# SyncE loads 32 table rows a quad instead of 20 in a graph attention kernel

## The chip, the cores and the metric

The kernel runs on one core of a Trainium2 chip. A core has a matrix engine (PE; its weight loads are listed apart as PEld), a vector engine (DVE), a scalar engine (ACT), a general engine (POOL) and a sequencer that only issues transfers and waits (SP). All of them run their own instruction streams in order and meet through semaphores. The metric is the device time of one execution in microseconds (us), as the median of several timed executions.

## The reference

The program is one graph attention layer with a residual. N = 12500 nodes have 128 features, E = 200000 edges come sorted by target node, and there are four heads of 32 channels:

```python
h   = relu(layernorm(x)) @ W_node.T            # a row per node, (H, HD)
e   = edge_features @ W_edge.T
att = sum(concat([h[src], h[dst], e]) * a)     # per edge and head
att = where(att > 0, att, 0.2 * att)
m   = max(segment_max(att, dst), 0)
ex  = exp(att - m[dst])
den = segment_sum(ex, dst) + (E - deg) * exp(-m)
out = x + segment_sum(ex / den[dst] * h[src], dst)
```

What matters here is `h[src]`: for every edge one row of the node table has to come to the edge's place. The sources are random, so each row is 548 scattered bytes (137 numbers of 4 bytes).

## The kernel before, in words

**Tiling.** The edges are cut into 392 groups of 511 (512 places with one carried in front), and four groups make a quad: 98 quads. A group has four chunks of 128 edges, one edge per partition, so a quad has 16 chunks. A first stage normalises the nodes and writes the node table to DRAM; then the quads are worked through.

**Three steps of a quad.** `logits(q, i)` makes the logits of group i of quad q: DVE compares targets (L612), PE multiplies (L618, L621). After some quads (a "super" of mostly four) `softmax` runs over them. `sums(q)` weighs the gathered rows (DVE, L925), marks the targets (DVE, L899) and lets PE add up rows by target (L964, and L841 for the carried row); ACT prepares columns for it (L893, L947), carries a row (L851) and takes the exponent for the division (L871), whose result DVE finishes (L1136). The functions are generators that are interleaved by hand: `together` takes one step of each in turn, so one step of logits of quad q + 5 stands beside one step of sums of quad q. In the late quads the same order holds, with windows of two groups (quads 36 to 74) and then of one (from 75), where earlier quads have one window for all four groups.

**How rows get to the edges.** The usual way is a gather: POOL issues one indirect transfer per chunk (L183). A ring of eight quads holds the rows (`ga`), and the gathers of quad q + 2 are issued when the logits of quad q begin. Some chunks go without a gather. `rows_for` picks them: one chunk of the last group of a quad, every 128 / a_quad quads, where a_quad is the number of rows that an engine is to load per quad. For these chunks `loaded_by_row` issues 128 transfers of one row each (L796), on ACT for one set of chunks and on SP for another. The addresses come from a list of sources (`of`, L782, loaded by SP), which DVE multiplies by the row's size (`at_row`, L789) and from which the engine loads a_quad registers at a time (L538). The rows land in one of three buffers of 128 rows; `take_rows` lets ACT wait for a chunk's count and copy it into the ring (L815) at the beginning of that quad's logits.

**When rows are issued.** `load_rows(by_sync, q, n)` advances SP's generator by n rows. It is called at the end of each of the four steps of logits with `BEHIND_LOGITS`, and at the end of each of the four steps of sums with `BEHIND_HOT`, both from quad 2 on. SP's chunks are set by

```python
sync_rows = rows_for((BEHIND_LOGITS + BEHIND_HOT) * QG, J - 2, SYNC_FROM + 6)
```

so the same two constants give the number of chunks.

**What else is in SP's queue.** SP issues, in the order of the program, the edge features of quad q + 2 (`ea`, L345), its targets (`db`, L351, after the last step of logits of quad q), its target rows (`pw`, L552), the inputs of the next quad (`inputs`, L552), the results (`out_dram`, L552, each waiting for DVE at L1136), rows for the softmax (`dr`, L592), and register loads (L538) for those whose place is computed. All of it, and the rows, run in one line.

Of the kernel before, what the change touches and what calls it, by code (L numbers as in the profile page):

```python
# [38 lines left out]
QUADS = 8  # L39
ROWS_FROM, ROWS_AHEAD, ROW_BUFS = 6, 7, 3  # L40
BEHIND_COUNT, BEHIND_SUMS, BEHIND_QUAD = 5, 1, 4
SYNC_FROM, BEHIND_LOGITS, BEHIND_HOT = 2, 3, 2
CLASSES = (22, 4, NARROW), (36, 4, WIDE), (75, 2, WIDE), (None, 1, NARROW)
FOLDS, PARTS = 1, 3
SETS = max(NODE_T, QG * J)
# [1500 lines left out]
```

## Time and profile before

| | |
|---|---|
| timed executions | 2762.9 us median of 3 (2750.94 to 2772.4) |
| the profiled execution | 2792.17 us, its span 2790.3 us |
| granted PE clock, mean | 0.531 of full speed |
| PE, PEld, DVE, ACT, POOL busy | 49%, 45%, 45%, 12%, 52% |
| rows loaded by ACT, by SP | 2304, 1664 |
| gathers from the table, from x | 1463, 72 |

The profile is of one execution. Its busy shares count work of the engines themselves; what a sequencer does (register loads, waiting, issuing transfers) is not busy time, so SP has no share at all and is read from the order of its issues and from its waits. PE's durations are modelled at full clock, while the clock granted to it is listed beside them. The waits put each idle stretch down to what ended it last; "remote" and "issue" are those where the profile names no engine. 1664 rows are 13 chunks of 128.

### The profile page before, as it was taken

The numbers are of one execution on the slowest core, as the hardware profiler recorded it, in microseconds if no ns is written. First come the engines' busy times: TensorE is split into PE (matmuls) and PEld (weight loads), VectorE is DVE, ScalarE is ACT, GpSimd is POOL, SyncE is SP. The second block draws the span as 40 slices with busy tenths as digits, with TensorE's granted clock in tenths as the row PEclk, the third lists the DMA queues.
The fourth block names the chain that finished last, engine by engine and source line by source line (L and its number), as shares of the span: only waits on it lengthen the run. The fifth ranks groups of instructions, "written<-read, shape, count | busy, mean of one in ns | idle before, by whom it ended". The sixth has DMA issues, their size and how long they took to land. (4 is left out here: it accounts for less than half of the span.)

```text
span 2790.3 us, 33673 instructions
## 1 busy us (share of the span) xinstructions
PE 1375.5 (49%) x7375; PEld 1256.4 (45%) x7375; DVE 1259.5 (45%) x3401; ACT 335.6 (12%) x1114; POOL 1458.8 (52%) x1550
## 2 busy tenths in 40 slices
PE   3655345344335334434555455555555545554565
PEld 3545344334334334434455454445444544443455
DVE  4543344234233334324445445545453553453476
ACT  3533000000000000000000000000000011111112
POOL 6455444544545444454556565565565556556611
PEclk8656555555555555555555555555555555555556
DMA  5533333333323333333444444444443443444430
GB/s 171 158 94 79 83 87 93 92 80 73 107 85 104 95 92 95 92 107 86 112 119 126 115 120 115 124 126 124 118 127 99 108 106 93 109 103 108 111 75 24
DMA packets 158894, 288.27 MB, mean 103 GB/s; under 512 B 62393, under 2 KB 106040, under 8 KB 148305
## 3 DMA queue, kind: packets, MB, share of 16 engines
q1 hardware_dynamic: 103262, 174.80, 20.8%
q0 software_dynamic: 49120, 107.44, 16.6%
q10 hardware_dynamic: 6306, 3.85, 0.6%
q8 instruction: 61, 1.00, 0.2%
q14 instruction: 145, 1.18, 0.2%
HBM read 268.72 MB, written 17.20 MB: 102 GB/s over the span
## 5 line engine op out<-in xcount | busy, mean ns | idle before, releaser
L183 POOL DMA_INDIRECT ga<-table,srci x1463 | 1381.1, 944 | 1177.3 <-PE acc L841 553.7
L964 PE MATMUL acc<-ga,hot 128*113 128x137 f32 (+1 forms) x2702 | 721.3, 442 | 693.3 <-issue 310.0
L964 PEld LDWEIGHTS acc<-ga,hot 128*113 128x113 f32 (+1 forms) x2702 | 595.4, 281 | 719.4 <-issue 323.9
L621 PE MATMUL lg<-wblk,ea 128*128 128x8 f32 x1568 | 406.7, 357 | 0.0
L621 PEld LDWEIGHTS lg<-wblk,ea 128*128 128x128 f32 x1568 | 379.1, 307 | 0.0
L618 PEld LDWEIGHTS <-at 112*128 112x128 bf16 (+1 forms) x1568 | 222.8, 167 | 249.8 <-DVE at L612 152.2
L925 DVE TENSOR_TENSOR ga<-ga,ex_ps 128x528 f32<-128x528 f32 x385 | 265.4, 690 | 20.3 <-PE ex_ps L753 12.7
L618 PE MATMUL lg<-pw,at 112*128 112x12 bf16 (+1 forms) x1568 | 171.0, 182 | 197.4 <-DVE at L612 134.6
L612 DVE TENSOR_TENSOR at<-const_ps,db 112x512 bf16<-112x512 f32 (+1 forms) x392 | 264.5, 675 | 6.9 <-DMA db<-in_dst_dram 5.6
L1124 DVE SCALAR_TENSOR_TENSOR den_of<-acc,den_of 113x4 f32<-113x4 f32 (+1 forms) x114 | 17.9, 157 | 521.9 <-ACT den_of L871 375.8
L899 DVE TENSOR_TENSOR hot<-const_ps,slot 128x448 f32<-128x448 f32 (+1 forms) x392 | 215.2, 550 | 0.0
L841 PE MATMUL acc<-ga,hot 128*81 128x137 f32 (+1 forms) x402 | 134.5, 437 | 106.3 <-ACT ga L851 85.4
L630 DVE TENSOR_REDUCE const_ps<-lg 128x64 f32<-128x192 f32 x98 | 35.2, 360 | 291.8 <-remote 255.3
L841 PEld LDWEIGHTS acc<-ga,hot 128*81 128x81 f32 (+1 forms) x402 | 95.0, 271 | 122.1 <-ACT ga L851 95.1
L871 ACT ACTIVATE den_of<-acc 113x4 f32<-113x4 f32 (+1 forms) x114 | 19.7, 173 | 994.0 <-remote 811.0
L753 PE MATMUL ex_ps<-ident,ex 64*128 64x64 f32 (+3 forms) x112 | 18.8, 317 | 184.7 <-ACT ex L747 146.8
L753 PEld LDWEIGHTS ex_ps<-ident,ex 64*128 64x128 f32 (+3 forms) x112 | 13.9, 210 | 187.6 <-ACT ex L747 148.6
L183 POOL DMA_INDIRECT ga<-in_x_dram,srci x72 | 68.7, 955 | 41.7 <-issue 21.1
L716 DVE TENSOR_TENSOR_SCAN ends<-thru,tops,ex_ps 1x16 f32<-1x16 f32 (+3 forms) x112 | 24.1, 216 | 118.9 <-remote 93.3
L441 PE MATMUL row_ps<-wcat,hT 128*128 128x137 f32 x198 | 45.5, 388 | 51.5 <-DVE hT L433 14.8
L687 DVE TENSOR_TENSOR t_ps<-t_ps,low 64x511 f32<-64x511 f32 (+3 forms) x28 | 19.3, 689 | 113.1 <-ACT low L684 113.1
L851 ACT COPY ga<-acc 1x133 f32<-1x133 f32 x175 | 44.8, 256 | 205.6 <-issue 116.8
(179 smaller groups left out, 1200.2 us busy)
## 6 DMA issues: line engine op xcount, KB each, us to landing
db<-in_dst_dram SPq DMA_DIRECT2D x53, 1024.0 KB
ea<-in_edge_t_dram SPq DMA_DIRECT2D x98, 512.0 KB
by_row<-table ACTq DMA_DIRECT2D x2304, 0.5 KB
db<-in_dst_dram SPq DMA_DIRECT2D x45, 640.0 KB
by_row<-table SPq DMA_DIRECT2D x1664, 0.5 KB
ga<-table,srci POOLq DMA_INDIRECT x1463
table<-row SPq DMA_DIRECT2D x9, 616.5 KB
xt<-in_x_dram SPq DMA_DIRECT2D x9, 576.0 KB
```

The costliest lines, as they stand in the source:

```text
L183: nc.gpsimd.indirect_dma_start(out=ga[:, i, j, 0:width], out_offset=None, in_=rows, in_offset=bass.IndirectOffsetOnAxis(ap=srci[:, g0 + i, ...
L441: nc.tensor.matmul(row_ps[:, t, :ROW], hT[:, t, :], wcat, start=True, stop=True)
L612: nc.vector.tensor_tensor(at[:span, i, :], node_ps[:span, w0 + i // k:w0 + i // k + 1].to_broadcast([span, GE]), db[:span, i, :], op=OP.is ...
L618: nc.tensor.matmul(lg[:, i, j].rearrange("p k h -> p (k h)"), at[:span, i, j * P:(j + 1) * P], sw, start=i + j == 0, stop=False, skip_grou ...
L621: nc.tensor.matmul(lg[:, i, 2 * w:2 * w + 2, 0, :], ea[:, i, w, :], wblk, start=False, stop=True, skip_group_check=True)
L630: nc.vector.tensor_reduce(st[:, :m], LG[q][:, :m].rearrange("p g j k h -> p g j h k"), AX.X, OP.add)
L753: nc.tensor.transpose(ex_ps[:, j * SBG * H:j * SBG * H + R], ex[:R, j * P:(j + 1) * P], ident[:R, :R])
L841: nc.tensor.matmul(acc, hot[:, i, 0, 0:acc.shape[0]], ga[:, i, 0, :], start=False, stop=stop)
L851: nc.scalar.copy(into, before[0:1, 0:R_CNT + 1])
L899: nc.vector.tensor_tensor(hot[:, i, :, 1:1 + span], lane_ps[:, 0:span].unsqueeze(1).to_broadcast([P, J, span]), slot[:, quads[q][0] + i, : ...
L925: engine.tensor_tensor(val, val, weight.unsqueeze(3).to_broadcast([P, J, H, HW]), op=OP.mult)
L964: nc.tensor.matmul(acc, hot[:, i, j, 0:1 + span], ga[:, i, j, :], start=new and j == (1 if carried else 0), stop=i % k > 1 and i % k == k ...
```

## The change

Two constants: SP issues four rows, and not three, at each step of logits, and four, and not two, at each step of sums. That is 4 x 4 + 4 x 4 = 32 rows a quad in place of 4 x 3 + 4 x 2 = 20.

```diff
-SYNC_FROM, BEHIND_LOGITS, BEHIND_HOT = 2, 3, 2
+SYNC_FROM, BEHIND_LOGITS, BEHIND_HOT = 2, 4, 4
```

`rows_for` now picks a chunk every 4 quads and not every 6.4, from quad 12 and not from quad 15: 22 chunks and not 13. Each of the nine chunks that are added loses its gather on POOL, and gets 128 row transfers and one list of sources on SP, one DVE instruction, and one ACT wait and copy. SP loads 32 registers at a time and not 20. Which chunks ACT loads does not change.

## The prediction

> **What bounds the kernel now.** First the page: how long, which engines, and what clock PE was given. Second the same by stretch.
>
> ```profile
> span 2790.3 us, 33673 instructions
> ...
> PE 1375.5 (49%) x7375; PEld 1256.4 (45%) x7375; DVE 1259.5 (45%) x3401; ACT 335.6 (12%) x1114; POOL 1458.8 (52%) x1550
> ...
> PEclk8656555555555555555555555555555555555556
> ```
>
> ```profile
> 300.00:1200.00 900.00, 382.88 (x2093) 355.27 (x2092) 333.02 (x842) 52.08 (x179) 440.02 (x467) 0.50 0.34 92
> 1300.00:2500.00 1200.00, 629.96 (x3301) 575.44 (x3300) 575.47 (x1484) 110.62 (x416) 706.02 (x748) 0.51 0.42 114
> ```
>
> No engine is busy for more than 52%, but PE's durations are modelled at full clock and the granted clock is 0.50 to 0.51. From 1300 to 2500 us the 629.96 us of PE become 629.96 / 0.51 = 1235 us in a stretch of 1200: PE has no time left there (a little is counted twice where matmuls overlap). From 300 to 1200 us it is 382.88 / 0.50 = 766 of 900. So I take PE as the bound of the second half and as nearly that in the first. Third the groups, for who waits for whom.
>
> ```profile
> L183 POOL DMA_INDIRECT ga<-table,srci x1463 | 1381.1, 944 | 1177.3 <-PE acc L841 553.7 <-issue 387.6 <-remote 159.0
> ...
> L612 DVE TENSOR_TENSOR at<-const_ps,db 112x512 bf16<-112x512 f32 (+1 forms) x392 | 264.5, 675 | 6.9 <-DMA db<-in_dst_dram 5.6 <-issue 1.2
> ...
> L947 ACT COPY ga<-xs 128x80 f32<-128x80 f32 x97 | 31.5, 325 | 39.4 <-DMA ga<-table,srci 20.0 <-issue 12.8 <-DMA rows<-in_dst_rows_dram 2.4
> ...
> L642 DVE TENSOR_TENSOR U<-const_ps,ga 128x64 f32<-128x64 f32 x98 | 26.1, 266 | 16.9 <-ACT ga L324 13.0 <-DVE const_ps L630 0.4
> ...
> L815 ACT COPY ga<-by_row 128x137 f32<-128x137 f32 x31 | 9.4, 303 | 103.7 <-issue 103.7
> ...
> L789 DVE TENSOR_SCALAR at_row<-of 1x128 int32<-1x128 int32 x31 | 6.8, 219 | 0.0
> ```
>
> POOL's gathers are not late. POOL itself waits 553.7 us for PE to be done with a ring buffer (L183, behind L841); the first reader of gathered rows, L642, has no gather among what its 16.9 us of waiting are put down to; L947 waits for gathers for 20.0 us in the whole span. Fourth, SP, which has no busy time: its waits from 1300 to 2500 us (the first answer), and from 300 to 1200 (the second), as total, number, longest.
>
> ```profile
> SPq L552 <- DMA pw<-side: 7.9, 10, 1.4
> SPq L552 <- DVE res L1136: 5.8, 3, 2.1
> SPq L552 <- DVE const_ps L630: 4.2, 2, 3.6
> ```
>
> ```profile
> SPq L552 <- DVE const_ps L630: 88.7, 6, 21.2
> SPq L345 <- remote: 80.3, 13, 16.3
> SPq L552 <- DVE res L1136: 52.4, 9, 12.1
> SPq L552 <- DVE at_row L789: 45.5, 3, 21.9
> ```
>
> The second list holds over 260 us of waiting in 900. The first has 33 rows, these three the longest, and adds to some 38 us in 1200: **in the second half SP runs without a pause**, though nobody waits for it but L612, once, for 5.6 us. Whether that is SP's real load decides this case. One quad of its queue, from one load of targets to the next (columns: start, time until the last issue's end, line, transfer, number):
>
> ```profile
> 1912.74 0.36 SPq L351 DMA_DIRECT2D db<-in_dst_dram  x1
> 1913.20 0.87 SPq L796 DMA_DIRECT2D by_row<-table  x3
> 1914.95 0.32 SPq L552 DMA_DIRECT2D inputs<-in_x_dram  x1
> 1915.45 0.34 SPq L552 DMA_DIRECT2D out_dram<-res  x1
> 1915.90 1.20 SPq L796 DMA_DIRECT2D by_row<-table  x2
> 1917.82 0.70 SPq L345 DMA_DIRECT2D ea<-in_edge_t_dram  x1
> 1919.97 0.00 SPq L552 DMA_DIRECT2D pw<-side  x1
> 1921.38 2.84 SPq L796 DMA_DIRECT2D by_row<-table  x3
> 1924.24 0.00 SPq L552 DMA_DIRECT2D inputs<-in_x_dram  x1
> 1924.32 0.55 SPq L796 DMA_DIRECT2D by_row<-table  x2
> 1925.23 0.06 SPq L552 DMA_DIRECT2D pw<-side  x1
> 1925.38 1.40 SPq L796 DMA_DIRECT2D by_row<-table  x3
> 1927.57 0.71 SPq L552 DMA_DIRECT2D out_dram<-res  x1
> 1929.02 7.42 SPq L796 DMA_DIRECT2D by_row<-table  x7
> 1936.54 0.36 SPq L351 DMA_DIRECT2D db<-in_dst_dram  x1
> ```
>
> A quad takes 1936.54 - 1912.74 = 23.8 us. The same kind of row costs 0.87 us for three at one place and 7.42 for seven at another; the same kind of load of inputs is issued in 0.32 us once and in 0.00 once. An issue of 56 KB that takes nothing is not an issue timed at its own moment. The same line, by kind (ns, least, median, most):
>
> ```profile
> L796 SPq MOVE by_row<-table x1664: 2/29/1407, 197.6 to 2496.9; - x185
> L796 SPq DMA_DIRECT2D by_row<-table x1664: 2/228/1394, 197.7 to 2497.0; - x185
> ```
>
> A register move, which touches no queue of transfers, takes 29 ns or up to 1407, and an issue 228 or 2. I read the dear stretches as records that come late and in bunches, so as a matter of the recording and not of SP's work. That is a reading, not a measurement.
>
> **The change, part by part.**
>
> *Removed: nine gathers* (22 chunks for 1664 / 128 = 13). 9 x 0.944 = 8.5 us of POOL go, and their pauses. POOL was waiting for buffers, so this is worth 0; after it POOL waits that much longer for PE. Bound on the other side: the 20.0 us that L947 waited for gathers, with 8.5 us, 28.5 us, if they all stood on the path and went.
>
> *Added: 9 x 128 = 1152 rows on SP, 12 a quad.* Clean price: 0.87 us for three, the last issue 0.23, so (0.87 - 0.23) / 2 = 0.32 a row, 3.8 us a quad. Registers: 32 at a time, not 20; twelve rows with one such load took
>
> ```profile
> 746.18 5.12 SPq L796 DMA_DIRECT2D by_row<-table  x12
> ```
>
> so (5.12 - 0.23) - 11 x 0.32 = 1.4 us a load, 0.07 a register, and 12 more are 0.8. Together 4.6 us a quad. Dear price: the 20 rows of the quad above took 0.87 + 1.20 + 2.84 + 0.55 + 1.40 + 7.42 = 14.3 us, 0.71 each, so 8.6 + 0.8 = 9.4 us. At the clean price SP's whole quad is 20 x 0.32 + 1.4 for rows, about 8 x 0.45 for the other transfers and 1 for their registers (an estimate from 0.32 to 0.36 an issue in the rows above, and the gaps), 12.4 us, and 17 us after the change, of 23.8: hidden behind PE. I take this, 0 us on the path. At the recorded price it is 23.8 + 9.4, and nothing hides it (first rival).
>
> *Queues passed.* The rows stand ahead of SP's loads of targets, features, inputs and results, which are for the next quad or the one after, so each may come 5 us later within a lead of a quad or more. Behind a wait of SP for `at_row` stand these same loads.
>
> *Added on DVE:* nine L789, 9 x 0.219 = 2.0 us; DVE is busy 575.47 us of 1200, so PE hides them (2.0 if not). Nine lists of sources more are nine issues on SP, like those above under 0.4 us each, in its slack.
>
> *Added on ACT:* nine waits and copies L815, 9 x 0.303 = 2.7 us. They stand in the path, as here before the carried row for which PE waits:
>
> ```profile
> 718.75 0.31 ACT L815 COPY ga<-by_row 128x137 f32<-128x137 f32 x1 [3.84 <-issue]
> 718.90 0.23 ACTq L796 DMA_DIRECT2D by_row<-table  x1
> 718.96 0.26 ACT L851 COPY ga<-acc 1x133 f32<-1x133 f32 x1
> ```
>
> The wait itself should be over: counting the calls in the program's order, a chunk's last row is issued 33 calls, of eight a quad, before it is taken, so four quads. The idle 103.7 / 31 = 3.3 us before each L815 is ACT's own issuing; were it new each time, 9 x 3.6 = 33 us.
>
> **Sum**, against the profiled execution: 0 for the gathers, 0 for SP, 0 for DVE, 2.7 for ACT: 2792.2 + 3 = 2795. That execution lies 29 us above the median of the timed ones, so for the median I add the same to it: 2762.9 + 3 = **2766 us**. About 1% is what a measurement of this kernel can tell from no change (2750.94 to 2772.4).
>
> **Rivals.**
>
> 1. *SP becomes the bound* (slower): its recorded pace is its real one. For: 38 us of waits in 1200, 0.8 a quad; L612's 5.6 us. Against: the moves of 1407 ns and issues of 2. It decides once SP's quad is longer than PE's 23.8 us, and it bites when DVE has to wait for targets (L612), after the lead of a quad is used up. Price: 1200 / 23.8 = 50 quads, from (4.6 - 0.8) x 50 - 24 = +166 to (9.4 - 0.8) x 50 - 24 = +406. I take +260, nearer to the low end, as a longer quad lengthens the clean stretches first: 3023 us.
> The Trainium skill, page "Perfetto Trace Analysis", section "What 'DMA-bound' means", calls a program bound by a DMA sequencer where the issuing engine's track is solid with issues; by that rule this rival would be the forecast. The waits of SP agree with it, the lack of waits for SP does not.
> Its page "NOTIFIC — the notification-queue block", section "10. Constraints, capacities, measured rates", says that writing such records costs an engine no cycles. By it the dear stretches would be SP's own and the sum would be 3023 too; no row here can show which.
>
> 2. *SP is late only in part*: half of the dearness is real. SP's quad is then (12.4 + 23.8) / 2 = 18.1 before, and with (4.6 + 9.4) / 2 = 7 more 25.1: over by 1.3, x 50 - 24 = +41, and up to +100 where the late quads, with more transfers each, are over by more. Taken: +70, 2833 us.
>
> 3. *Faster*: gathers are on the path after all, and all 28.5 us go: 2734 us. For: L947's 20.0 us. Against: 553.7 us of POOL waiting for buffers.
>
> 4. *It does not do what it says.* The counts follow from the same constants, so this is no more than a chunk.
>
> **Chances.** Hidden, 2766 (own range 2750 to 2785): 0.55. SP the bound, 3023: 0.25. In part, 2833: 0.14. Faster, 2734: 0.06. So faster by over 1% 0.06, within 1% 0.55, slower by over 1% 0.39. The range takes the first case, the third, and the lower half of the second: 2742 to 3030, which leaves out about 0.16.
>
> **What would show it.** L183 x1454, SP's rows x2816, L815 and L789 x40. If I am right, the median stays within 1%, L612's wait for targets stays small in the timed pace, and PE's busy time over clock still fills the second half. SP's waits from 300 to 1200 us should shrink. If the first rival is right, L612 waits for `db` by tens or hundreds of us between 1300 and 2500, the clock being the same, and quads there last 27 us or more. What would make me wrong beside these: a wait of ACT at L815 that is new, with PE behind it at L841.

## The result and the profile after

The changed kernel takes 2977.57 us (median, 2961.45 to 2984.73) where the kernel before takes 2767.65 us (2750.94 to 2779.68): a ratio of 1.074, 95% interval 1.0667 to 1.0814. It is slower by 210 us. The profiled execution took 2961.45 us, 169 us more than the profiled one of before. In the experiments further below, the same kernel before took 1981 to 1984 us and not 2767, so their times are compared only with each other; what differs there is part of the finding.

First the page of the changed kernel, for the same lines as before.

```profile
span 2959.7 us, 36007 instructions
...
PE 1370.6 (46%) x7375; PEld 1251.7 (42%) x7375; DVE 1264.6 (43%) x3410; ACT 337.3 (11%) x1123; POOL 1449.7 (49%) x1541
...
PEclk8656555555555555555555555555555555555556
```

Every engine does nearly the same work as before (nine gathers fewer, nine copies more) at the same clock, and the span is longer: the time went into waiting. The table of two stretches says which half it went to.

```profile
300.00:1200.00 900.00, 375.76 (x2085) 350.85 (x2085) 332.36 (x843) 52.05 (x179) 434.25 (x461) 0.51 0.33 92
1300.00:2500.00 1200.00, 562.12 (x2940) 512.70 (x2939) 517.27 (x1336) 95.56 (x356) 627.77 (x667) 0.50 0.36 102
```

From 300 to 1200 us PE gets nearly as much done as before (375.76 us of work against 382.88). From 1300 to 2500 it gets 562.12 done, not 629.96. The groups of the changed kernel, with their idle time and what ended it, name the wait:

```profile
L183 POOL DMA_INDIRECT ga<-table,srci x1454 | 1372.1, 944 | 1356.1 <-PE acc L841 742.3 <-issue 374.7 <-remote 153.4
...
L612 DVE TENSOR_TENSOR at<-const_ps,db 112x512 bf16<-112x512 f32 (+1 forms) x392 | 265.1, 677 | 367.8 <-DMA db<-in_dst_dram 359.4 <-issue 8.2
...
L947 ACT COPY ga<-xs 128x80 f32<-128x80 f32 x97 | 31.4, 324 | 24.2 <-DMA ga<-table,srci 12.9 <-issue 6.8 <-DVE kp L665 0.4
...
L815 ACT COPY ga<-by_row 128x137 f32<-128x137 f32 x40 | 11.7, 302 | 85.8 <-issue 72.1 <-DVE hot L899 6.0 <-DVE at_row L789 5.4
```

L612, which compares targets, waits 359.4 us for the load of `db`; before it was 5.6. POOL waits more for PE, not less, so the gathers aren't late. ACT idles less before L815 than before (85.8 us and not 103.7, with nine copies more), so no new wait for rows shows. How L612's wait reaches PE stands at L618, which multiplies what L612 made; first the kernel before, then the changed one.

```profile
L618 PE MATMUL lg<-pw,at 112*128 112x12 bf16 (+1 forms) x1568 | 171.0, 182 | 197.4 <-DVE at L612 134.6
L618 PE MATMUL lg<-pw,at 112*128 112x12 bf16 (+1 forms) x1568 | 170.3, 181 | 445.7 <-DVE at L612 362.4
```

`db` is issued by SP. SP's waits from 1300 to 2500 us, the three longest of the list:

```profile
SPq L552 <- DMA pw<-side: 4.3, 6, 0.7
SPq L538 <- DVE U L642: 1.8, 1, 1.8
SPq L552 <- DMA inputs<-in_x_dram: 1.4, 2, 0.7
```

The list names next to nothing that SP waits for (17 us in all), and now others wait for SP. How complete such a list is in these two traces is taken up further below. How long its round is follows from the loads of `db` in the same stretch (one line of the source; least, median and longest duration in ns, first and last start); first the kernel before, then the changed one.

```profile
L351 SPq DMA_DIRECT2D db<-in_dst_dram x47: 2/347/712, 1310.3 to 2489.2; - x47
```

```profile
L351 SPq DMA_DIRECT2D db<-in_dst_dram x42: 2/362/785, 1316.3 to 2489.0; - x42
```

Before, (2489.2 - 1310.3) / 46 = 25.6 us a quad; after, (2489.0 - 1316.3) / 41 = 28.6. One quad of SP's queue in the changed kernel, the middle left out:

```profile
1909.38 0.01 SPq L351 DMA_DIRECT2D db<-in_dst_dram  x1
1910.11 3.57 SPq L796 DMA_DIRECT2D by_row<-table  x4
...
1916.98 1.25 SPq L796 DMA_DIRECT2D by_row<-table  x4
...
1924.26 4.96 SPq L796 DMA_DIRECT2D by_row<-table  x4
...
1934.33 8.03 SPq L796 DMA_DIRECT2D by_row<-table  x12
1942.46 0.36 SPq L351 DMA_DIRECT2D db<-in_dst_dram  x1
```

Dear and cheap stretches stand side by side as before: four rows take 1.25 us here and 4.96 there.

### The profile page after: what moved, and what is told of

Same layout as the page of the kernel before. It is cut to its first block, busy times and chain, and to the rows that moved or that the text cites. A ratio compares the mean times of both kernels' runs of the same rounds, so it can differ in the third digit from the quotient of the medians.

```text
span 2959.7 us, 36007 instructions
## 1 busy us (share of the span) xinstructions
PE 1370.6 (46%) x7375; PEld 1251.7 (42%) x7375; DVE 1264.6 (43%) x3410; ACT 337.3 (11%) x1123; POOL 1449.7 (49%) x1541
## 5 line engine op out<-in xcount | busy, mean ns | idle before, releaser
L183 POOL DMA_INDIRECT ga<-table,srci x1454 | 1372.1, 944 | 1356.1 <-PE acc L841 742.3
L964 PE MATMUL acc<-ga,hot 128*113 128x137 f32 (+1 forms) x2702 | 719.5, 442 | 691.4 <-issue 278.1
L964 PEld LDWEIGHTS acc<-ga,hot 128*113 128x113 f32 (+1 forms) x2702 | 594.3, 280 | 716.9 <-issue 292.6
L618 PEld LDWEIGHTS <-at 112*128 112x128 bf16 (+1 forms) x1568 | 217.8, 165 | 503.9 <-DVE at L612 389.5
L612 DVE TENSOR_TENSOR at<-const_ps,db 112x512 bf16<-112x512 f32 (+1 forms) x392 | 265.1, 677 | 367.8 <-DMA db<-in_dst_dram 359.4
L618 PE MATMUL lg<-pw,at 112*128 112x12 bf16 (+1 forms) x1568 | 170.3, 181 | 445.7 <-DVE at L612 362.4
L183 POOL DMA_INDIRECT ga<-in_x_dram,srci x72 | 68.6, 953 | 41.2 <-issue 21.1
L874 ACT COPY pt<-acc 81x137 f32<-81x137 f32 x88 | 23.7, 269 | 344.4 <-PE acc L841 151.9
```

The source lines that it names most:

```text
L183: nc.gpsimd.indirect_dma_start(out=ga[:, i, j, 0:width], out_offset=None, in_=rows, in_offset=bass.IndirectOffsetOnAxis(ap=srci[:, g0 + i, ...
L612: nc.vector.tensor_tensor(at[:span, i, :], node_ps[:span, w0 + i // k:w0 + i // k + 1].to_broadcast([span, GE]), db[:span, i, :], op=OP.is ...
L618: nc.tensor.matmul(lg[:, i, j].rearrange("p k h -> p (k h)"), at[:span, i, j * P:(j + 1) * P], sw, start=i + j == 0, stop=False, skip_grou ...
L964: nc.tensor.matmul(acc, hot[:, i, j, 0:1 + span], ga[:, i, j, :], start=new and j == (1 if carried else 0), stop=i % k > 1 and i % k == k ...
```

## The experiments

**More rows, fewer rows.** The first two change only the constants, to 24 and to 28 rows a quad:

```diff
-SYNC_FROM, BEHIND_LOGITS, BEHIND_HOT = 2, 4, 4
+SYNC_FROM, BEHIND_LOGITS, BEHIND_HOT = 2, 3, 3     # 24 rows
+SYNC_FROM, BEHIND_LOGITS, BEHIND_HOT = 2, 3, 4     # 28 rows
```

> 24 rows a quad on SP, three at each step of logits and of sums: 16 chunks by rows. The changed kernel pays 4.9 us in each quad from about quad 48 to quad 88, for 12 rows more than before. Theory A (SP's issuing is the bound, at its recorded pace of about 0.7 to 0.8 us a row, and SP had some spare time before): there is a threshold. Twelve rows at 0.78 us are 9.4 us, of which 4.9 came through, so 4.5 us a quad were spare; four rows at 0.78 are 3.1 us, less than that, so no loss: 2740 to 2790 us. Theory B (the copies on ACT, the waits for a chunk, or the register loads cost it, so the price goes by the chunk): three of nine chunks, a third of +210: about 2835 us. Theory C (SP had only the 0.8 us a quad of waits that the profile of before shows, and a row costs 5.7 / 12 = 0.47 us): +1.1 us in 40 quads, about 2810 us.

> 28 rows a quad on SP, three at each step of logits and four at each of sums: 19 chunks by rows. Theory A (threshold at 4.5 us a quad, 0.78 us a row): eight rows are 6.2 us, 1.7 over, in some 40 quads +70: about 2835 us. Theory B (by the chunk): six of nine, two thirds of +210: about 2905 us. Theory C (0.8 us spare, 0.47 us a row): +3.0 us in 40 quads, about 2885 us.

Measured: the kernel before 1981.66 us; 24 rows 1979.23 (ratio 0.9984, 0.9972 to 0.9995), 28 rows 1982.75 (1.0007, 0.9993 to 1.002). No loss shows at all, where 32 rows cost 1.0% at this pace (next run), so at this pace nothing goes by the chunk (B, a third and two thirds of it) or by a flat price of every row (C). The 0.2% that 24 rows gain is less than executions of one kernel differ by (1976.45 to 1986.23 us for the kernel before). The 70 us that A gave 28 rows don't show either: its spare time was reckoned from another pace, since the kernel before takes 786 us less here. So the first reading is of the pace itself: the rows on SP in the kernel with 24.

```profile
L796 SPq MOVE by_row<-table x2048: 29/29/38, 136.5 to 1767.1; - x187
L796 SPq DMA_DIRECT2D by_row<-table x2048: 227/228/581, 136.5 to 1767.2; - x187
```

A register move takes 29 to 38 ns and never 1407, an issue 227 to 581 and never 2. The dear stretches and the issues of nothing are gone together, and with them 28% of the time.

**The changed kernel at this pace.** It was run again as it is.

> The changed kernel again, unchanged. In the runs of 24 and 28 rows the kernel before took 1981 us, where it had taken 2767 us in the comparison of the change: the chip, or the state it is in, sets how dear an instruction of SP is (0.34 us a row there, 0.5 to 0.7 us here before). Theory A (SP's issues, at the price of the moment): where the kernel before takes 1980 us, a row costs 0.34 us and a quad 19.5 us; SP with 24 rows was busy some 15.6 us of it, so with 32 rows it is busy 15.6 + 8 x 0.34 + 0.6 = 18.9 us, just under the quad: within 1.5% of the kernel before, 1970 to 2010 us. Where the kernel before takes 2760 us, it is 7% slower again, 2950 to 2985 us. Rival (copies, waits, fewer gathers, register loads: costs that don't depend on the price of an issue): 4.9 us a quad in either place, so about 2150 us where the kernel before takes 1980.

Measured: 2001.47 us against 1982.83, ratio 1.0099 (1.0064 to 1.0134). Not 2150: theory A's figure holds. The same four lines of the groups and the window read now:

```profile
L183 POOL DMA_INDIRECT ga<-table,srci x1454 | 1374.0, 945 | 446.9 <-issue 343.2 <-DMA ga<-table,srci 33.0 <-PE acc L964 32.9
L964 PE MATMUL acc<-ga,hot 128*113 128x137 f32 (+1 forms) x2702 | 718.7, 441 | 245.6 <-ACT ga L947 150.9 <-DVE hot L899 58.0 <-issue 13.9
...
L612 DVE TENSOR_TENSOR at<-const_ps,db 112x512 bf16<-112x512 f32 (+1 forms) x392 | 264.5, 675 | 35.2 <-DMA db<-in_dst_dram 35.1
...
L642 DVE TENSOR_TENSOR U<-const_ps,ga 128x64 f32<-128x64 f32 x98 | 26.1, 266 | 213.4 <-DMA ga<-table,srci 196.0 <-issue 8.0 <-ACT ga L324 7.1
```

```profile
300.00:1200.00 900.00, 617.05 (x3336) 573.02 (x3335) 555.35 (x1434) 93.52 (x333) 678.75 (x720) 0.51 0.53 151
```

The instructions themselves last as long as in the comparison of the change (L183 945 ns and 944, L612 675 and 677). What is short now is the time between them: PE at L964 idles 13.9 us for "issue", where the changed kernel idled 278.1 in the comparison. L612 still waits for `db`, 35.1 us, and POOL gathers almost without a pause (343.2 of its 446.9 us of idle time are its own issuing), so that L642 waits 196.0 us for gathers. And one quad of SP's queue is clean from end to end:

```profile
1200.63 0.36 SPq L351 DMA_DIRECT2D db<-in_dst_dram  x1
1201.09 1.24 SPq L796 DMA_DIRECT2D by_row<-table  x4
...
1211.93 0.34 SPq L552 DMA_DIRECT2D out_dram<-res  x1
1214.53 3.89 SPq L796 DMA_DIRECT2D by_row<-table  x12
1218.51 0.36 SPq L351 DMA_DIRECT2D db<-in_dst_dram  x1
```

Twelve rows in 3.89 us are (3.89 - 0.23) / 11 = 0.33 us a row; the round is 1218.51 - 1200.63 = 17.9 us, the register load of 32 (2.1 us, before the twelve rows) in it.

**Half the issues, all the rest.** SP fetches two neighbouring rows with one issue; every second row of these chunks is then the next row of the table and not the source's.

```diff
-                    row = engine.dma_start(as_bytes(to[p:p + 1, :]),
-                                           rows_at(table, at[p % a_quad], 4 * ROW, 1))
+                    both = 1 if j == J - 1 else 2
+                    if p % both == 0:
+                        row = engine.dma_start(as_bytes(to[p:p + both, :]),
+                                               rows_at(table, at[p % a_quad], 4 * ROW, both))
...
```

> The changed kernel, with SP's rows fetched two to an issue: each issue takes the even row and the row that follows it in the table, so half of the rows of these chunks are not the right ones. The bytes, the chunks by rows (22), the copies and waits on ACT, the removed gathers and the registers loaded (32 a quad) stay as in the changed kernel; SP's issues of rows are halved, 16 a quad and not 32. Theory A (the number of issues on SP): SP has less to do than in the kernel before, so the loss is gone whole: 2740 to 2785 us, and the wait of L612 for the targets is under 20 us. Theory B (copies, waits, register loads or the removed gathers): it stays where the changed kernel is, 2950 to 2985 us.

Measured: 1974.47 us, ratio 0.9957 (0.9941 to 0.9974). The wait of L612 for targets is 0.1 us. Bytes, copies, register loads and the removed gathers are those of the changed kernel, so of its 1.4% against this one, all goes with the number of issues or with what is halved along with them (the register moves of SP and the transfers themselves). What is left, 7 us of gain, is of the size of nine gathers at 0.945 us and 0.29 between them (11 us). The wait fell as theory A said; its microseconds were those of the other pace.

**All the gathers and all the rows.** POOL gathers the 22 chunks as well, and the loaded rows are copied aside.

```diff
-                if (q, i, j) in by_row:
+                if (q, i, j) in by_row and j != J - 2:
                     continue
...
-                taken = nc.scalar.copy(GA[q][:, i, j, :], to)
+                into = GA[q][:, i, j, :]
+                if j == J - 2:
+                    into = work.tile([P, ROW], BF16, name="unused", bufs=1)
+                taken = nc.scalar.copy(into, to)
```

> The changed kernel, with the 22 chunks that SP loads also gathered by POOL: SP issues its 32 rows a quad as before, ACT waits for them and copies them aside (in bf16, into a tile that nobody reads), and the sums use POOL's gathered rows. So no gather is taken away (23 more than in the changed kernel's POOL queue is the most, 1476 in all), and ACT's part is the same. Theory A (SP's issues alone): as slow as the changed kernel, 2950 to 3000 us, at the upper end if SP's pace is slow whenever POOL gathers, since POOL gathers for some 21 us more. Rival (the slowdown comes from the gathers that went, by the order in which buffers come free or by what POOL does in their place): as the kernel before, 2740 to 2785 us.

Measured: 2025.08 us, ratio 1.0217 (1.02 to 1.0235). The expectation's microseconds were those of the other pace; by its rule, as slow as the changed kernel or a little slower, it held. Against the changed kernel, 22 gathers more (1476, not 1454) cost 2025.08 - 2001.47 = 24 us, 1.07 each: at this pace a gather is on the path, nearly with its whole time.

**No gathers.** The changed kernel without POOL's gathers from quad 8 on.

```diff
-                if (q, i, j) in by_row:
+                if (q, i, j) in by_row or q >= QUADS:
                     continue
```

> The changed kernel without POOL's gathers from quad 8 on: the rows that POOL gathers are left as they are in the ring buffer, so most of the sums are wrong. SP's and ACT's rows, copies and waits stay. Where the kernel before takes 1980 us: POOL, which there issues gathers without a pause (0.945 us each and 0.29 us between), is taken off, and SP's 18.9 us a quad is the next bound: 1850 to 1960 us; if POOL is not the bound there, no change from the changed kernel. Where the kernel before takes 2760 us: if SP's dear stretches come from POOL's gathers (they began 3 to 4 us after POOL started a run of gathers), a row costs 0.34 us and SP is under its quad: below 2700 us; if they come from the chip's state alone, SP stays dear and the time stays at 2900 us or more.

Measured: 1940.24 us, ratio 0.9782 (0.9763 to 0.9801), inside the 1850 to 1960 that were expected if SP is the next bound. Most of the sums are wrong in this kernel, since the gathered rows are missing. With POOL away SP is the next bound, and the sign of it is the one from the comparison:

```profile
L612 DVE TENSOR_TENSOR at<-const_ps,db 112x512 bf16<-112x512 f32 (+1 forms) x392 | 264.8, 676 | 150.1 <-DMA db<-in_dst_dram 149.9
```

One idea on the dear stretches falls here: in the comparison they began soon after POOL started a run of gathers. SP's register moves from 600 to 1500 us, with POOL gathering almost without a pause (the changed kernel) and then with POOL idle (this one):

```profile
L796 SPq MOVE by_row<-table x1476: 29/29/38, 601.9 to 1499.6; - x185
```

```profile
L796 SPq MOVE by_row<-table x1568: 29/29/38, 600.6 to 1499.7; - x196
```

The longest is 38 ns in both, against 1407 in the comparison. Gathers alone don't make SP's instructions dear.

**Each row a little dearer.** A register load that nobody uses was put ahead of every second row, in both kernels; in a third, the targets were also loaded by ACT's queue.

```diff
+                    if kind == mybir.EngineType.SP and p % 2 == 0:
+                        windows(at_row, 4 * ROW, p, 1, kind)
                     row = engine.dma_start(as_bytes(to[p:p + 1, :]),
```

```diff
-            nc.sync.dma_start(db[:n, :m, :], dst.rearrange("(g e) -> g e", e=GE)[g0:g0 + m]
+            queue = nc.scalar if q >= 2 else nc.sync
+            queue.dma_start(db[:n, :m, :], dst.rearrange("(g e) -> g e", e=GE)[g0:g0 + m]
```

> The kernel before, its rows on SP made dearer by hand: ahead of every second row SP loads one register more, which nobody uses. Such a load takes 0.27 us in the traces and some 0.03 us to the next instruction, so a row costs about 0.15 us more, 0.49 and not 0.34 us. Theory A (what counts is whether SP's quad, rows x price and the rest, is longer than the others' quad): where the kernel before takes 1980 us, SP with 24 rows was busy 15.6 us of a quad of 19.5, so with 20 it is busy 14.2, and dearer 14.2 + 20 x 0.15 = 17.2 us: still hidden, 1975 to 2000 us. Rival (every instruction more on SP delays its loads and is felt): 20 x 0.15 = 3 us in some 78 quads, 2210 us.

> The changed kernel with the same register loads ahead of every second row of SP, so 0.49 us a row, near the 0.5 to 0.7 us that the traces of the first comparison show. Theory A: SP's quad is 18.9 + 32 x 0.15 = 23.7 us where the others need 19.4, so every quad from about 10 to 88 is 4.3 us longer, and L612 waits for the targets by hundreds of us: 1998 + 78 x 4.3 to 4.8 = 2330 to 2375 us, 17% or more above the kernel before, while the same dearness leaves the kernel before as it is. Rival (the loss of 7% was a thing of that chip's ACT, PE or memory and not of SP's issues): 2000 to 2050 us.

> The dear changed kernel, with the targets (L351) loaded by ACT's queue and not by SP's, from quad 2 on. If the place of the targets in SP's queue is what costs (they alone stand too late), the loss goes: 2000 to 2050 us. If SP's whole work in a quad is the bound, another of its loads is late in their place (features L345, windows' weights or inputs L552, or a chunk's rows at L815), and only the 0.4 to 0.5 us of that issue is won, some 35 us in 78 quads: 2295 to 2345 us.

Measured: 1982.4 us (1.0002, 0.9988 to 1.0015), 2054.93 (1.0359, 1.0334 to 1.0384) and 2043.29 (1.0299, 1.028 to 1.0319). The dose was not the one meant. In the changed kernel's trace the loads are missing, and a semaphore step stands in their place:

```profile
L538 SPq EVENT_SEMAPHORE  x1413: 17/17/853, 132.2 to 1902.8; - x177
...
L538 SPq TENSOR_LOAD <-at_row x88: 1875/2127/2242, 133.3 to 1882.7; - x88
```

Such a step takes 0.06 us to the next instruction, so it is 0.03 us a row: 832 x 0.064 = 53 us more for SP in the kernel before, of which nothing came through, and 1408 x 0.064 = 90 us in the changed kernel, of which 2054.93 - 2001.47 = 53 did. The forecasts of 2330 and 2295 us were for another dose and are missed; the asymmetry, which the theory is about, is there. L612 waits 252.5 us for targets. With the targets on ACT's queue that wait is gone (0.1 us for L612 in all), yet only 12 us are won. (The 2043 us lie in the range of the other case, 2000 to 2050, but with so small a dose that says nothing.) DVE waits for SP to send results off instead; in the list of waits of the third kernel, whose lines stand three lower at this place (L1139 is L1136):

```profile
DVE res L1139 <- DMA out_dram<-res: 81.0, 33, 5.2
DVE res L1162 <- DMA out_dram<-res: 75.2, 10, 11.7
```

So it isn't the place of `db` alone: the other transfers that SP issues are late too. How much of the time that is left is ACT's, which now issues `db`, this run doesn't tell.

**Loads moved at the plain price.** The changed kernel with the targets and the features on ACT's queue (the second diff, and the same for L345).

> The changed kernel at the plain price of a row, with the targets (L351) and the features (L345) loaded by ACT's queue. SP's quad falls by two issues of 0.40 us and their waits, from 18.9 to about 18.0 us. If SP is just at its limit with 32 rows (the wait of L612 for targets, 35 us in the changed kernel where the kernel before takes 1980), the 20 us of loss go, and the nine gathers that went show as a gain of up to 9 x 1.24 = 11 us: 1970 to 1985 us. ACT's two issues, 0.8 us a quad, stand partly in the path: if wholly, +65 us: 2040.

Measured: 2004.18 us, ratio 1.0105 (1.0088 to 1.0123), the changed kernel's own 1.0099 within the interval. L612 waits for nothing, SP has pauses (52.6 us in its longest item from 600 to 1500 us), U at L642 waits 131.0 us for gathers: SP is relieved and the loss stays, so the 1970 to 1985 us of the first case were missed; the time lies between them and the 2040 of the second. ACT's two issues a quad take the place of SP's lateness, or the gathers do; the run doesn't tell which.

**A row at the recorded price.** SP's addresses come into registers two at a time, and not 20 or 32.

```diff
-                    if p % a_quad == 0:
-                        at = windows(at_row, 4 * ROW, p, min(a_quad, P - p), kind)
+                    few = 2 if kind == mybir.EngineType.SP else a_quad
+                    if p % few == 0:
+                        at = windows(at_row, 4 * ROW, p, min(few, P - p), kind)
                     row = engine.dma_start(as_bytes(to[p:p + 1, :]),
-                                           rows_at(table, at[p % a_quad], 4 * ROW, 1))
+                                           rows_at(table, at[p % few], 4 * ROW, 1))
```

> The register loads that were added ahead of every second row before left no load in the program, only a semaphore's step of 0.06 us each, so that dose was 0.03 us a row. Now the kernel before, with SP's row addresses loaded into registers two at a time and not 20: 832 loads of some 0.35 us (a load of one register took 0.27 us, 32 took 2.13, so 0.06 for each more) with 0.06 us to the next instruction, in place of 91 of 1.45: SP has 832 x 0.41 - 91 x 1.45 = 209 us more to issue, 2.3 us a quad, and a row costs about 0.46 us with its share of the load and not 0.41. Theory A: where the kernel before takes 1980 us its SP is busy 14.2 us of 19.5, so 16.5 is still hidden: 1975 to 2000 us. Rival (each instruction more on SP is felt): 2190 us.

> The changed kernel with the same loads of two registers and not 32: 1408 x 0.41 - 88 x 2.2 = 384 us more for SP. Theory A: SP has no time to spare with 32 rows (90 us of semaphore steps more cost 54 us of time there, 0.6 us each, and nothing in the kernel before), so 0.6 to 1.0 of the 384 us come through: 2230 to 2385 us, with L612 waiting for targets by some 400 us, a quad about 4 us longer, as in the first comparison, and the kernel before unmoved by the same. Rival (the slowdown of 7% has to do with something else that is dear on that chip): 2050 us, no more than the small dose gave.

Measured: the kernel before 2053.24 us (1.0347, 1.0328 to 1.0366), the changed one 2844.11 us (1.4338, 1.4313 to 1.4363). The dose is again not the one meant, this time more than double, so the forecasts of 1975 to 2000 and of 2230 to 2385 us are both missed. The loads of the kernel before, and then of the changed one:

```profile
L538 SPq TENSOR_LOAD <-at_row x832: 467/730/938, 131.6 to 1811.0; - x167
```

```profile
L538 SPq TENSOR_LOAD <-at_row x1408: 473/726/994, 132.7 to 2695.8; - x176
```

A load of two takes 0.73 us and not 0.35. With 0.05 us to the next instruction a row then costs 0.33 + 0.78 / 2 = 0.72 us: just the 0.71 that the prediction read from the dear stretches. In SP's time that is 832 x 0.78 - 91 x 1.51 = 512 us more for the kernel before, of which 70 came through, and 1408 x 0.78 - 88 x 2.18 = 906 us for the changed one, of which 843 did. So the kernel before had some 440 us of SP's time to spare, 4.9 us in each of some 90 quads, and the changed kernel some 60, 0.7 a quad. In the kernel before with loads of two, L612 waits 319.9 us for `db`, though only 70 us are lost: SP is at its limit there too, and a wait at L612 is not all lost time. The wait is the one of the comparison, in the changed kernel with loads of two:

```profile
L612 DVE TENSOR_TENSOR at<-const_ps,db 112x512 bf16<-112x512 f32 (+1 forms) x392 | 265.5, 678 | 1088.4 <-DMA db<-in_dst_dram 1088.4
```

The rival of 2050 us for it is out. But a row at 0.72 us does not make the kernel before slow: it takes 2053 us with such rows, and not 2767. So dear rows on SP alone are not what the comparison had.

## Why the prediction was wrong in its likeliest case

The likeliest case, 2766 us with SP's rows hidden, didn't happen. The first rival did: SP became the bound, through L612 waiting for `db`, between 1300 and 2500 us, at the same clock, with quads over 27 us. All its signs are in the profile after. The median, 2978 us, lies between the 3023 us of that rival and the 2833 us of the second (late only in part). It lies in the stated range, 2742 to 3030, only because the range takes in most of the way to that rival, which had a chance of 0.25. That is a wide range and not a right mechanism. The third (gathers on the path) has nothing for it in the comparison: L947's wait for gathers was 20.0 us and is 12.9. The fourth falls with the counts, which are the expected ones (L183 x1454, L815 x40).

**The step that failed** is the reading of the dear stretches: "I read the dear stretches as records that come late and in bunches, so as a matter of the recording and not of SP's work." The single stamps are odd, since an issue of 56 KB in 2 ns is no issue at its own moment. But the sum of them is time that SP spent in these executions. L612's idle time, which is stamped on DVE, grew from 6.9 to 367.8 us, 359.4 of it for a load that SP issues, and where the dear stretches are absent the same change costs 1.0% and not 7.4%.

That the recording is the cause of these stretches is neither shown nor ruled out. The two traces of the comparison lack records: the changed kernel's holds 21018 updates of semaphores, and that of the same kernel run again holds 52236, with 36007 instructions in both. The kernel before has 16573, the kernel with the semaphore steps, which is nearly the same program, 50969. If the recording held the sequencers up there, the prediction was right about the cause and wrong in leaving its time out. The times don't settle it. Each execution of the changed kernel has a span and a granted clock on record, so none is known to have run unrecorded, and the fully profiled execution is the quickest of the changed kernel (2961 us, the others 2975 to 2985) but the slowest of the kernel before (2792, the others 2751 to 2780).

The lack of records bears on the waits of SP, since a wait of SP is listed only where the update that ended it was kept. The spare time of SP stood in the quoted rows: 38 us of waits in 1200, 0.8 us a quad, but that is a least value. Summed from the trace, the time between SP's last instruction and one that waits for a semaphore is 127 us in the same stretch, 2.7 us in each of 47 quads, which is a most value (in the changed kernel it is 60 us, where the list names 17). Either is less than the 4.6 us that the change was reckoned to add, and that should have carried the case. The missing wait for SP in the profile before, on which the forecast leant, says that SP isn't yet late, and nothing of how near it is.

**The size.** Rival 1 had a low end of (4.6 - 0.8) x 50 - 24 = 166 us, from the clean price, a high end of 406 from the dear one, and a value taken of 260. The profiled executions differ by 169 us, the medians by 210. So the added rows cost about what clean rows cost, although the rows beside them were dear; that 166 and 169 are so near each other is partly luck. A quad grew from 25.6 to 28.6 us between 1300 and 2500 us, by 3.0, where 4.6 - 0.8 = 3.8 was reckoned, so some 1.6 us a quad were spare. The 23.8 us that the prediction took for a quad were those of one quad.

**The clean price** was right. Twelve rows take 3.89 us where the stretch is clean (0.33 a row, 0.32 was taken), a load of 32 registers 2.13 us (32 x 0.07 = 2.2 was reckoned), and SP's quad 17.9 us (17 was reckoned). At the pace of the experiments the rows are then nearly hidden, as the likeliest case had it, with 1.0% left.

**PE as the bound** was wrong. The prediction divided PE's busy time by its granted clock and took the stretch as full. By the same division the changed kernel at the pace of the experiments has 617.05 / 0.51 = 1210 us of PE in a stretch of 900. That can't be, so the division isn't allowed with these durations, and nothing in the comparison shows PE full.

**The gathers** were worth nothing in the comparison, as said: POOL's wait for PE grew from 553.7 to 742.3 us. At the pace of the experiments POOL is the engine without a pause, and a gather is worth 1.07 us. **ACT**: the nine copies cost nothing that shows. **SP's waits from 300 to 1200 us** shrank as said, the longest item from 88.7 to 17.0 us:

```profile
SPq L552 <- DVE const_ps L630: 17.0, 7, 6.1
```

That is why this half paid next to nothing: there SP had pauses to fill.

The rule of the Trainium skill, page "Perfetto Trace Analysis", section "What 'DMA-bound' means", that a solid issuing track marks the bound, fits the changed kernel as far as the waits go: SP's list names next to nothing and L612 waits for SP. Its page "NOTIFIC — the notification-queue block", section "10. Constraints, capacities, measured rates", says that emitting the record of an instruction costs the engine no cycles. No run here shows that, since none is known to have run without records.

What makes the sequencers' instructions dear in the comparison and not in the experiments stays open. It isn't the gathers alone (the changed kernel run again has them and no dear stretch), and by the durations it isn't the engines' own instructions. The experiments ran on four chips, and the kernel before took 1981 to 1984 us on each; the chip of the comparison isn't on record, so the chip may be the cause, too. No run here had the dear stretches and took away one thing.

## What to carry to other kernels

A queue that issues is read as an engine: its time from one round to the next, less its waits, is its load, however odd the single stamps look, and its waits are all it has to spare. A list of waits shows them only where the records that ended them were kept, so the number of records is worth a look. Work moved to a queue costs nothing up to that spare time and most of its price beyond it: 53 us of extra instructions cost the kernel before nothing, 90 cost the changed one 53, and 906 cost it 843. Whether the spare time is there can depend on the pace of the moment, so a change that fills a queue to its limit is a risk even where it measures 1%.

## What the runs showed of the hardware

- The same program took 2978 us in one place and 2001 us in the other (the changed kernel; the kernel before 2767 and 1981 to 1984), at nearly the same mean granted clock (0.528 and 0.540 in the profiled executions) and with the same duration of each engine's instructions (L183 944 and 945 ns). What differs in the traces is the sequencers and the records: a register move on SP took up to 1485 ns in the one and at most 38 in the other, and 21018 updates of semaphores were kept in the one and 52236 in the other.
- A load of two registers (0.73 us) costs half of one of 20 (1.46, the kernel with the semaphore steps) and a third of one of 32 (2.13). From 20 to 32 it is 0.056 us a register; below 20 the slope doesn't hold, since it would give 1.46 - 18 x 0.056 = 0.45 us for two. The Trainium skill, page "DMA: Bandwidth & Descriptors", section "Latency and other measured facts", gives such a load a floor of about 600 ns. The median of the loads of two, 730 ns, lies above it, but the least is 467 ns, and other register loads of SP in the same trace took as little as 264 ns, so 600 ns is no floor here.
- A register load whose value isn't used leaves no load, but a semaphore step of 17 ns, 0.06 us to the next instruction. On a queue with almost no spare time that was enough to be seen: 2.7% for 1408 of them.
